# Running the last block's filter taps inside the last recurrence steps of a fused attention, GRU and convolution kernel

## The chip, the cores and the metric

The kernel runs on one core of one Trainium2 chip. The metric is the device time of one execution in microseconds; the time before is 1845.0 us, the median of three executions (1844.51 to 1854.32).

## What is computed

Four residual stages follow one another on an input `x` of shape (4, 512, 512) (batch, time, feature) with a conditioning vector of shape (4, 512). The first is an attention with 16 heads, the second a recurrence over the 512 time steps, the third and fourth depthwise causal convolutions whose four weights per feature are the conditioning vector's four rows:

```python
x = x + attention(x, cond)            # 16 heads, RMS norms, output projection
x = x + gru(cond, x)                  # 512 steps, one after the other
x = x + causal_conv(x, w=cond)        # 4 taps per feature
x = x + causal_conv(x, w=cond) + b    # 4 taps per feature, and a bias
```

The recurrence is sequential: a step needs the state of the step before. The two convolutions with their residuals are together one filter with seven taps per feature (k = 0 to 6), so output time t needs the sum of attention output and state at the times t-6 to t.

## The kernel before, in words

The time axis is cut into 16 blocks of 32 steps. One loop over the 512 steps (`for t in range(T)`) runs the recurrence, and beside it a list scheduler (`Queue`) writes the other work into the instruction streams in small pieces: the attention of later blocks, and the filter of the block before. The order in each engine's queue is the order in which the program emits instructions; nothing is moved afterwards. Each engine works its queue in that order.

**One recurrence step.** TensorE multiplies the state with the weights (L1250: 32 matmuls into X, 32 into Y). VectorE transposes X (L1264, tile TX) and adds (L1266, S). ScalarE takes the tanh (L1267, ZT), reseeds X for the next step (L1139) and forms D (L1270). VectorE transposes Y (L1276) and scans (L1277), ScalarE takes the second tanh (L1278), and VectorE's scans write the new state, A (L1287) in half and HS (L1288) in full precision. `prep` then makes the operands of the next step: BX on VectorE (L1149) and ScalarE (L1151), BY on GpSimd (L1150) and ScalarE (L1152), HH on GpSimd (L1154). Last, GpSimd adds the new state to the attention output X1 and writes column 6 + t % 32 of a history buffer `x2b` (L1292). `x2b` has 38 columns per row: six from the block before, and 32 of the block.

**The filter of a block** (`conv_tasks`). Task C1 has stages that `q_.head` emits at the start of a step, right behind `prep` and L1292 of the step before and in front of the step's own work on VectorE, ScalarE and GpSimd. `f1` (L1175) starts the sum in a tile `x4` with tap 0 and the bias: four ScalarE instructions, one for each group j of 128 features, which read columns 0 to 31 of `x2b`. Tap k then adds columns k to k+31, either on VectorE with one instruction for each group (`tap`, L1183), or on GpSimd with two (`tap_p`, L1190 and L1191). Tap k so reads column 31 + k last, which is the state of step 25 + k of the block. Task TX transposes the result on TensorE (L310, tile px), copies it on ScalarE to a tile `ob` (L1209) and sends it out with one DMA of 256 KB on SyncE's queue (L1210). `ob` is allocated with the tag of `x4`, and that tag has one buffer. The counter `cv` (one) lets C1 of a block start only when TX of the block before has been emitted.

For blocks 0 to 14 the filter is spread over the steps of the next block, all its taps on GpSimd (24 pairs). For block 15 there is no next block: its C1 is made behind the loop and flushed, with three groups' taps on VectorE (18 instructions) and one group's on GpSimd (6 pairs).

**The scheduler's limits.** A stage is emitted in a step if its planned cost fits into what is left of the engine's budget in that step (`DVE_B, ACT_B, POOL_B = 1130, 1900, 3300`), or if the whole budget of that engine is left. Tasks are looked at in the order of their priority: TX of block 14 comes ahead of C1 of block 15. A task's next stage comes at the earliest one step later.

Of the kernel before, what the change touches and what calls it, by code (L numbers as in the profile page):

```python
# [15 lines left out]
B, T, D, H = 4, 512, 512, 16  # L16
P = 128
NB = T // 32
# [12 lines left out]
PR = dict(LX=(86, 0), XH=(-226, 0), Q=(-27, 0), R=(-389, 0), ON=(-294, 0),  # L31
          TO=(-110, 0), WO=(-65, 0), GI=(-82, 0), C1=(130, 0),
          TX=(130, 0), LK=(159, 1.1), S=(4, 4.8), TP=(52, 4.7), AV=(115, 2.6))
# [138 lines left out]
def body(ctx, tc, x, cond, W_emb, b_emb, g_norm, W_qkv, g_q, g_k, W_out, W_ih, W_hh, b_ih, b_hh, L3_b, out):  # L172
# [13 lines left out]
    def pm(name):  # L186
        return pb.tile([P, 512], F32, name=name, tag="m", bufs=2)
# [128 lines left out]
    def lt(name, shape, dt=F32, bufs=1, tag=None):  # L316
        return lat.tile(shape, dt, name=name, tag=tag or name, bufs=bufs)
# [11 lines left out]
    q_ = Queue(dict(m=2, s=3, O=1, P=4, PT=4, xb=3, xhl=1, QS=3, q=1, o=1, gi=1, x1=3, L=3))  # L329
# [788 lines left out]
    f = lambda a: a.rearrange("p a k -> p (a k)")  # L1118
# [22 lines left out]
    def seedY(t):  # L1141
        nc.scalar.activation(Y, G[(t // 4) % 2][:, t % 4, 2, :], AF.Copy)
# [24 lines left out]
    def conv_tasks(i):  # L1167
        s = {}
        a = x2b[i % 2]

        def f1(jp):
            if jp == 0:
                s["x4"] = lt("x4", [P, D])
            for j in (2 * jp, 2 * jp + 1):
                nc.scalar.activation(s["x4"][:, 128 * j:128 * j + 128].rearrange("p (b t) -> p b t", b=4), a[:, 4 * j:4 * j + 4, 0:32],  # L1175
                                     AF.Identity, scale=VC[:, j, 0:1], bias=l3T[:, j:j + 1])

        def tap(k, jp, js=None):
            def g():
                x4 = s["x4"].rearrange("p (a t) -> p a t", t=32)  # L1180
                for j in js or (2 * jp, 2 * jp + 1):
                    J = slice(4 * j, 4 * j + 4)
                    nc.vector.scalar_tensor_tensor(x4[:, J, :], a[:, J, k:k + 32], VC[:, j, k:k + 1], x4[:, J, :], ALU.mult, ALU.add)  # L1183
            return g

        def tap_p(k, j):
            def g():
                tm = lt("tm", [P, 4, 32], bufs=2)
                o = s["x4"].rearrange("p (a t) -> p a t", t=32)[:, 4 * j:4 * j + 4, :]
                nc.gpsimd.tensor_scalar(tm, a[:, 4 * j:4 * j + 4, k:k + 32], VC[:, j, k:k + 1], 1.0, ALU.mult, ALU.mult)  # L1190
                nc.gpsimd.tensor_tensor(o, tm, o, ALU.add)  # L1191
            return g

        C1 = Task(f"C1{i}", prio=100 * i + PR["C1"][0],
                  stages=[[("ACT", 700, lambda jp=jp: f1(jp))] for jp in range(2)] + ([
                      [("Pool", 900, tap_p(k, j))] for k in range(1, 7) for j in range(4)] if i < NB - 1 else [
                      [("Pool", 900, tap_p(k, 3)), ("DVE", 526, tap(k, 0)), ("DVE", 300, tap(k, 1, (2,)))] for k in range(1, 7)]),
                  acq=["cv"], rel=["x1"])

        def toc(j):  # L1200
            def f():
                if j == 0:
                    s["px4"] = pm("px4")
                transpose4(s["px4"], s["x4"], (j,))
            return f

        def tos():
            ob = lt("ob", [P, D], tag="x4")
            nc.scalar.activation(ob, s["px4"], AF.Copy)  # L1209
            nc.sync.dma_start(out[:, 32 * i:32 * i + 32, :], ob)  # L1210

        TX = Task(f"TX{i}", prio=100 * i + PR["TX"][0], deps=[C1], acq=["m"], chunks=[(150, toc(j)) for j in range(4)], stages=[[("ACT", 480, tos)]], rel=["m", "cv"])
        return [C1, TX]

    q_.free["cv"] = 1
    CT = {}
# [6 lines left out]
    with tc.manual_schedule(engines={ENG.PE, ENG.DVE, ENG.Activation, ENG.Pool, ENG.SP}):  # L1223
        seed_first(0, 0)
        Bx, By, HH = prep(A, HS, 0)
        due = None
        for t in range(T):
            i = t // 32
            zt, d0 = ZT[t % 2], D0[t % 2]
            if t % 32 == 0:  # L1230
                if i == 0:
                    taps_()
                else:
                    q_.flush(CT.get(i - 2, []))
                    CT[i - 1] = conv_tasks(i - 1)
                    q_.add(CT[i - 1])
            if t % 4 == 0 and t + 4 < T:
                due = t // 4 + 1
            if due and due % 8 == 0 and (t % 4 == GI_T or all(u.done is not None and u.done <= q_.step for u in need[due // 8])):
                q_.flush(need[due // 8])  # L1240
                load_g(due)
                due = None
            elif due and due % 8:
                load_g(due)
                due = None
            q_.head(dict(DVE=DVE_B, ACT=ACT_B, Pool=POOL_B))

            def mm(dst, lhs, M, W, k, cols):
                for qq in range(4):
                    nc.tensor.matmul(dst[32 * qq:32 * qq + M, :], lhs, W[:, k, cols].rearrange("p g (j q s) -> p q g j s", j=4, q=4)[:, qq], start=False, stop=True,  # L1250
                                     skip_group_check=True)

            for k in range(4):
                mm(X, A[:, 4 * k:4 * k + 4, 1], 4, Wlo, k, slice(0, 2))
            for k in range(4):
                mm(X, Bx[:, k].rearrange("p s b -> p (s b)"), 8, Whi, k, slice(0, 2))
            if t == 0:
                seed_first(0, 1)
            for k in range(4):
                mm(Y, By[:, k].rearrange("p b s -> p (b s)"), 16, Wlo, k, slice(2, 3))  # L1260
            for k in range(4):
                mm(Y, By[:, k].rearrange("p b s -> p (b s)"), 16, Whi, k, slice(2, 3))
            TX = wk.tile([P, 8, 32], F32, name="TX", tag="TX", bufs=1)
            nc.vector.transpose(TX.rearrange("p a r -> p (a r)"), X)  # L1264
            S = wk.tile([P, 64], F32, name="S", tag="S", bufs=1)[:, 0:32]
            nc.vector.tensor_tensor(S.rearrange("p (a b) -> p a b", a=8), TX[:, :, 0:4], TX[:, :, 4:8], ALU.add)  # L1266
            nc.scalar.activation(zt[:, :, :, 2], S.rearrange("p (g a) -> p g a", g=2), AF.Tanh, scale=0.5 * IWS)  # L1267
            if 1 < t + 1 < T:
                seedX(t + 1)
            nc.scalar.activation(d0[:, :, 1], zt[:, 1, :, 2], AF.Copy, scale=-0.5, bias=0.5)  # L1270
            D1 = wk.tile([P, 16, 2], F32, name="D1", tag="D1")
            An = wk.tile([P, 16, 2], F16, name="A", tag="A")
            HSn = wk.tile([P, 16, 2], F32, name="HS", tag="HS")

            TY = wk.tile([P, 2, 4, 4, 4], F32, name="TY", tag="TY", bufs=2)
            nc.vector.transpose(TY.rearrange("p h j b k -> p j h (b k)"), Y.rearrange("p (j h r) -> p j h r", j=4, h=2))  # L1276
            nc.vector.tensor_tensor_scan(f(NN), f(zt[:, 0]), TY[:, 0].rearrange("p j b k -> p (j b k)"), 0.0, ALU.mult, ALU.add)  # L1277
            nc.scalar.activation(D1[:, :, 0], NN[:, :, 3], AF.Tanh, scale=0.5 * IWS)  # L1278
            nc.vector.scalar_tensor_tensor(D1[:, :, 1], zt[:, 1, :, 2], 1.0, HH, ALU.add, ALU.mult)
            if 1 < t + 1 < T:  # L1280
                seedY(t + 1)
            if t == 0:
                seed_first(1, 0)
                seed_first(1, 1)
            q_.pe(SLOT0 if t < NS0 else PE_SLOT, INS0 if t < NS1 else PE_INS, (PART, 1e9))
            keep_warm(-(-(WARM - q_.cols) // 384), pm("warm")[:, 0:384] if q_.free["m"] else None)
            nc.vector.tensor_tensor_scan(f(An), f(d0), f(D1), 0.0, ALU.mult, ALU.add)  # L1287
            nc.vector.tensor_tensor_scan(f(HSn), f(d0), f(D1), 0.0, ALU.mult, ALU.add)  # L1288
            A, HS = An, HSn
            if t + 1 < T:  # L1290
                Bx, By, HH = prep(A, HS, t + 1)
            nc.gpsimd.tensor_tensor(x2b[i % 2][:, :, 6 + t % 32], X1[i].rearrange("p (a t) -> p a t", t=32)[:, :, t % 32], HS[:, :, 1], ALU.add)  # L1292
            if t % 32 == 31 and i + 1 < NB:
                nc.gpsimd.tensor_scalar(x2b[(i + 1) % 2][:, :, 0:6], x2b[i % 2][:, :, 32:38], 1.0, 1.0, ALU.mult, ALU.mult)
            q_.step += 1
        ct = conv_tasks(NB - 1)
        q_.add(ct)
        q_.flush(ct)


_INS = ["x", "cond_2048", "L0_cond_W_emb", "L0_cond_b_emb", "L0_cond_g_norm", "L0_cond_W_qkv", "L0_cond_g_q",
# [20 lines left out]
```

## Time and profile before

| what | value |
|---|---|
| median of three executions | 1845.0 us |
| the profiled execution: its own time | 1849.01 us |
| its span in the trace | 1846.9 us |
| TensorE busy (matmul) | 1575.0 us, 85% |
| VectorE busy | 1237.8 us, 67% |
| ScalarE busy | 1200.5 us, 65% |
| GpSimd busy | 767.5 us, 42% |
| mean granted TensorE clock | 0.989 |
| last recurrence step: first matmul | 1828.41 us |
| its new state HS written | 1831.45 us |
| last VectorE tap ended | 1838.75 us |
| DMA of the last output block issued | 1840.15 us |

Busy time is counted for each engine by itself, and the engines run at the same time; a share of 85% does not say that this engine sets the end. Here the loop over the steps is a chain that goes through all engines, so the table's lower half matters more for this change: it shows the end of the program, where nothing but the last block's filter and its output is left. The times of the steps are counted from the span's start. In this profile step 506 (`t = T - 6`) has its first matmul at 1813.54 us, and the steps 507 to 511 at 1816.51, 1819.51, 1822.48, 1825.44 and 1828.41 us.

### The profile page before, as it was taken

The numbers are of one execution on the slowest core, as the hardware profiler recorded it, in microseconds if no ns is written. First come the engines' busy times: TensorE is split into PE (matmuls) and PEld (weight loads), VectorE is DVE, ScalarE is ACT, GpSimd is POOL, SyncE is SP. The second block draws the span as 40 slices with busy tenths as digits, with TensorE's granted clock in tenths as the row PEclk, the third lists the DMA queues.
The fourth block names the chain that finished last, engine by engine and source line by source line (L and its number), as shares of the span: only waits on it lengthen the run. The fifth ranks groups of instructions, "written<-read, shape, count | busy, mean of one in ns | idle before, by whom it ended". The sixth has DMA issues, their size and how long they took to land.

```text
span 1846.9 us, 116397 instructions
## 1 busy us (share of the span) xinstructions
PE 1575.0 (85%) x49019; PEld 1159.2 (63%) x49019; DVE 1237.8 (67%) x4774; ACT 1200.5 (65%) x4701; POOL 767.5 (42%) x2850
## 2 busy tenths in 40 slices
PE   4889988899998989898989999898989898987554
PEld 2444566666766767676666667676766676765442
DVE  4785467576767676777677676766666777665555
ACT  4664466767676767677776767676767677755543
POOL 1255023252535444443535353545444453434343
PEclk9989999999999999999999999999999999999998
DMA  5662011101010101010100111010101000011000
GB/s 175 224 209 116 21 54 28 41 17 34 17 35 19 35 27 44 18 30 25 28 24 24 29 46 30 19 35 17 36 13 35 17 25 25 18 28 29 18 12 16
DMA packets 68937, 78.26 MB, mean 42 GB/s; under 512 B 6560, under 2 KB 54720, under 8 KB 67776
## 3 DMA queue, kind: packets, MB, share of 16 engines
q1 hardware_dynamic: 68416, 70.82, 12.6%
q8 instruction: 387, 6.34, 1.5%
q14 instruction: 134, 1.10, 0.2%
HBM read 44.58 MB, written 26.21 MB: 38 GB/s over the span
## 4 chain that ended last, share of the span: by engine, by line
PE 43%; DVE 21%; ACT 19%; issue 7%; DMA 4%; POOL 4%; SPq 1%; ACTq 0%; DVEq 0%; POOLq 0%
PE X L1250 23%; DVE TX L1264 7%; ACT X L1139 6%; PE ps L457 5%; DVE A L1287 4%; PE Y L1250 4%; ACT D L1278 4%; DVE S L1266 3%; PE ptp L310 2%; PE pgi L590 2%; ACT PX L473 2%; ACT D L1270 2%; PE pkv L949 2%; PE po L501 1%; ACT ZT L1267 1%
## 5 line engine op out<-in xcount | busy, mean ns | idle before, releaser
L1150 POOL TENSOR_TENSOR BY<-HS,A 128x32 f16<-128x32 f32 x512 | 127.2, 248 | 854.7 <-DVE HS L1288 799.6
L1250 PE MATMUL X<-Wlo,A 128*4 128x256 f16 x8192 | 312.6, 272 | 158.7 <-DVE A L1287 150.1
L1267 ACT ACTIVATE ZT<-S 128x32 f32<-128x32 f32 x512 | 133.3, 260 | 425.6 <-DVE S L1266 425.0
L1264 DVE STREAM_TRANSPOSE TX<-X 128x256 f32<-128x256 f32 x512 | 230.4, 450 | 257.0 <-PE X L1250 256.8
L1250 PEld LDWEIGHTS <-A 128*4 128x4 f16 x8192 | 151.9, 83 | 263.9 <-DVE A L1287 221.5
L1250 PE MATMUL X<-Whi,BX 128*8 128x256 f16 x8192 | 314.9, 273 | 0.9 <-issue 0.8
L1250 PEld LDWEIGHTS <-BY 128*16 128x16 f16 x16384 | 276.2, 90 | 35.4 <-issue 13.3
L1250 PE MATMUL Y<-Wlo,BY 128*16 128x128 f16 x8192 | 208.9, 219 | 11.6 <-POOL BY L1150 7.2
L1250 PE MATMUL Y<-Whi,BY 128*16 128x128 f16 x8192 | 209.9, 219 | 2.8 <-issue 2.4
L1250 PEld LDWEIGHTS <-BX 128*8 128x8 f16 x8192 | 180.8, 86 | 49.7 <-ACT BY L1152 3.9
L1139 ACT ACTIVATE X<-G 128x256 f32<-128x256 f32 x510 | 201.7, 396 | 5.3 <-DMA G<-GD 4.4
L473 ACT ACTIVATE PX<-ps,nb,rqs 128x512 f32<-128x512 f32 x256 | 195.4, 764 | 9.4 <-DVE nb L465 7.0
L1287 DVE TENSOR_TENSOR_SCAN A<-D,D 128x32 f16<-128x32 f32 x512 | 115.6, 226 | 122.9 <-ACT D L1278 121.9
L464 DVE TENSOR_REDUCE mx<-ps 128x1 f32<-128x512 f32 x256 | 174.6, 684 | 22.1 <-PE ps L457 22.0
L1277 DVE TENSOR_TENSOR_SCAN N<-ZT,TY 128x64 f32<-128x64 f32 x512 | 150.0, 293 | 58.7 <-ACT ZT L1267 7.8
L1191 POOL TENSOR_TENSOR x<-tm,x 128x128 f32<-128x128 f32 x366 | 166.6, 455 | 31.0 <-POOL tm L1190 0.6
L1276 DVE STREAM_TRANSPOSE TY<-Y 128x128 f32<-128x128 f32 x512 | 158.5, 310 | 17.5 <-PE Y L1250 7.7
L310 PE MATMUL ptp<-ident,PX 128*128 128x128 f32 x1024 | 165.2, 281 | 1.4 <-ACT PX L473 0.6
L501 PEld LDWEIGHTS po<-V,PT 128*32 128x32 f32 x8192 | 107.6, 111 | 77.9 <-issue 70.0
L501 PE MATMUL po<-V,PT 128*32 128x32 f32 x8192 | 147.9, 199 | 5.7 <-issue 4.9
L493 ACT ACTIVATE PT<-ptp 128x512 f32<-128x512 f32 x248 | 143.7, 582 | 11.0 <-PE ptp L310 10.9
L1151 ACT ACTIVATE BX<-A 128x16 f16<-128x16 f16 x512 | 110.8, 216 | 61.0 <-DVE A L1287 1.5
(268 smaller groups left out, 3074.5 us busy)
## 6 DMA issues: line engine op xcount, KB each, us to landing
GD<-gs SPq DMA_DIRECT2D x45, 256.0 KB
G<-GD SPq DMA_DIRECT2D x512, 16.0 KB
G<-GD SPq DMA_DIRECT2D x512, 8.0 KB
xp<-in_x_dram SPq DMA_DIRECT2D x16, 256.0 KB
xb<-in_x_dram SPq DMA_DIRECT2D x16, 256.0 KB
xhl<-XD SPq DMA_DIRECT2D x32, 128.0 KB
out_dram<-ob SPq DMA_DIRECT2D x16, 256.0 KB
wst<-in_L_cond_W_qkv_dram SPq DMA_DIRECT2D x6, 512.0 KB
```

The costliest lines, as they stand in the source:

```text
L310: nc.tensor.transpose(dst[:, 128 * j:128 * j + 128], src[:, 128 * j:128 * j + 128], ident)
L464: nc.vector.tensor_reduce(s["mx"][:, h:h + 1], s[("s", j, q)], AX.X, ALU.max)
L473: nc.scalar.activation(pe_, s[("s", j, q)], AF.Exp, bias=s["nb"][:, h:h + 1], scale=s["rqs"][:, h:h + 1], accum_out=s["ls"][:, h:h + 1])
L501: nc.tensor.matmul(s["po"][32 * b:32 * b + 32, 32 * h:32 * h + 32], s["PT"][h][:, kt, 32 * b:32 * b + 32], V[:, 4 * b + kt, 32 * h:32 * h ...
L1139: nc.scalar.activation(X.rearrange("p (g c) -> p g c", g=2), G[(t // 4) % 2][:, t % 4, 0:2, :], AF.Copy)
L1191: nc.gpsimd.tensor_tensor(o, tm, o, ALU.add)
L1250: nc.tensor.matmul(dst[32 * qq:32 * qq + M, :], lhs, W[:, k, cols].rearrange("p g (j q s) -> p q g j s", j=4, q=4)[:, qq], start=False, st ...
L1264: nc.vector.transpose(TX.rearrange("p a r -> p (a r)"), X)
L1267: nc.scalar.activation(zt[:, :, :, 2], S.rearrange("p (g a) -> p g a", g=2), AF.Tanh, scale=0.5 * IWS)
L1276: nc.vector.transpose(TY.rearrange("p h j b k -> p j h (b k)"), Y.rearrange("p (j h r) -> p j h r", j=4, h=2))
L1277: nc.vector.tensor_tensor_scan(f(NN), f(zt[:, 0]), TY[:, 0].rearrange("p j b k -> p (j b k)"), 0.0, ALU.mult, ALU.add)
L1287: nc.vector.tensor_tensor_scan(f(An), f(d0), f(D1), 0.0, ALU.mult, ALU.add)
```

## The change

Only block 15's filter is changed. Its C1 is put into the scheduler at step 506 (26 of the block) in place of behind the loop. There `f1` becomes one stage of four instructions. One stage follows for each of the taps 1 to 5: groups 0 and 1 on VectorE, groups 2 and 3 on GpSimd. Tap 6 has groups 0, 1 and 2 on VectorE and group 3 on GpSimd. With one stage for each step, `f1` comes at the head of step 506, taps 1 to 5 at the heads of steps 507 to 511, and tap 6 is flushed behind the loop.

```diff
-        C1 = Task(f"C1{i}", prio=100 * i + PR["C1"][0],
-                  stages=[[("ACT", 700, lambda jp=jp: f1(jp))] for jp in range(2)] + ([
-                      [("Pool", 900, tap_p(k, j))] for k in range(1, 7) for j in range(4)] if i < NB - 1 else [
-                      [("Pool", 900, tap_p(k, 3)), ("DVE", 526, tap(k, 0)), ("DVE", 300, tap(k, 1, (2,)))] for k in range(1, 7)]),
-                  acq=["cv"], rel=["x1"])
+        if i < NB - 1:
+            st = [[("ACT", 700, lambda jp=jp: f1(jp))] for jp in range(2)] + [[("Pool", 900, tap_p(k, j))] for k in range(1, 7) for j in range(4)]
+        else:
+
+            st = [[("ACT", 1400, lambda: (f1(0), f1(1)))]] + [
+                [("DVE", 526, tap(k, 0)), ("Pool", 900, tap_p(k, 2)), ("Pool", 900, tap_p(k, 3))] for k in range(1, 6)] + [
+                [("DVE", 526, tap(6, 0)), ("DVE", 300, tap(6, 1, (2,))), ("Pool", 900, tap_p(6, 3))]]
+        C1 = Task(f"C1{i}", prio=100 * i + PR["C1"][0], stages=st, acq=["cv"], rel=["x1"])
...
+            if t == T - 6:
+                CT[NB - 1] = conv_tasks(NB - 1)
+                q_.add(CT[NB - 1])
             q_.head(dict(DVE=DVE_B, ACT=ACT_B, Pool=POOL_B))
...
-        ct = conv_tasks(NB - 1)
-        q_.add(ct)
-        q_.flush(ct)
+        q_.flush(CT[NB - 1])
```

## The prediction

> **What bounds the kernel now.** I read the chain of waits first. Up to the last step it is the recurrence, about 2.97 us a step and through every engine; behind it the chain, asked for the last 22 us, is the filter of the last block on VectorE, then its output (columns: start us, length us, what):
>
> ```profile
> 1828.41 1.07 PE X L1250 x32
> ...
> 1831.52 4.11 DVE x L1183 x11
> 1835.63 0.41 issue
> 1836.04 1.06 DVE x L1183 x3
> 1837.10 0.24 issue
> 1837.34 0.90 DVE x L1183 x2
> 1838.23 0.14 issue
> 1838.37 1.14 PE px L310 x4
> 1839.53 0.60 ACT ob L1209
> ```
>
> So 7.23 us of taps (18 on VectorE, 1831.52 to 1838.75) stand bare at the end. That bounds the gain: it can't be more than 0.4% of the time. A difference of 0.5% (9.2 us) is about what a measurement of this kernel can tell from no change.
>
> Next the timeline, at single records of the taps (start us, length us):
>
> ```profile
> 1837.34 0.62 DVE L1183 SCALAR_TENSOR_TENSOR x<-x2b,VC,x 128x128 f32<-128x128 f32 x1
> 1838.41 0.34 DVE L1183 SCALAR_TENSOR_TENSOR x<-x2b,VC,x 128x128 f32<-128x128 f32 x1
> ```
>
> The first ran beside a GpSimd add (L1191), the second with GpSimd idle. Beside GpSimd's multiply a tap takes 0.45 us. Alone, taps follow one another in 0.27 us; beside GpSimd's pairs (0.925 us each) two fit into a pair, 0.46 us each.
>
> **What the change removes.** Behind the loop only tap 6 is left. In the clock of the old trace: GpSimd's last column (L1292) is written at 1831.77. VectorE's three taps then start at about 1831.83, 2.20 and 2.66 (the first beside GpSimd's multiply, the second beside its add, the third mostly with GpSimd idle) and end at 1833.05; GpSimd's pair ends at about 1832.7. The old transposes ended 0.74 us behind the last tap (1838.75 to 1839.49), the new ones then end at 1833.79. The gain is 1839.49 - 1833.79 = **5.7 us**. Copy and output behind it are the same. The transposes in the middle of the loop, at full clock, took 0.67 us for four against 1.12 at the end, so if the clock is still up another 0.2 goes; I leave it out.
>
> **What it adds at step 506.** f1 goes to ScalarE's queue right behind block 14's copy to `ob` (planned 480 + 1400 of 1900, so it fits), and in front of the step's tanh. f1 writes `x4`, which lives in the one buffer that `ob` has. It must wait until block 14's output DMA has read `ob`. Before, f1 came 16.6 us after that DMA's issue (1814.37 to 1830.98), and nothing waited. The timeline shows copy and tanh; the DMA view, asked from the issue at 1814.37 for 12 us (slices of 0.3 us), shows the transfer:
>
> ```profile
> 1813.76 0.58 ACT L1209 ACTIVATE ob<-px 128x512 f32<-128x512 f32 x1
> 1815.35 0.26 ACT L1267 ACTIVATE ZT<-S 128x32 f32<-128x32 f32 x1 [1.01 <-DVE S L1266]
> ```
> ```profile
> DMA  0000271301212222210000002000000000000001
> ```
>
> Packets move until slice 18, 5.6 us after the issue. The same transfer at the very end is waited for, so its completion is seen. This line is from the waits of SyncE's queue (us, times, longest):
>
> ```profile
> SPq L1315 <- DMA out_dram<-ob: 5.2, 1, 5.2
> ```
>
> Issued at 1840.15 and 0.55 long, plus 5.2: completion 5.75 us after issue. So f1 can start at 1814.37 + 5.75 = 1820.12. Four instructions at a pitch of 0.385 (1830.98, 1831.37, 1831.75, 1832.13 in the old tail) hold ScalarE until 1821.7, where the tanh stood ready for 1815.35. Everything else of the step hangs on that tanh: **+6.35 us**. Bounds: without any wait f1 would start when column 31 is there (1814.37) and end at 1815.95, +0.6; with the slowest of the 16 output transfers in this trace, whose stretch has packets until 8.3 us after issue (other loads among them), +9.0. I take 5.75, since both transfers with nothing beside them (blocks 14 and 15) end in the same slice.
>
> The Trainium skill, page "DMA: Bandwidth & Descriptors", section "Anatomy of one DMA — SWDGE (gpsimd) path", gives a transfer as about 2 us fixed plus bytes over 436 GB/s, for GpSimd's queue. By that 256 KB would take 2.6 us, step 506 would lose 3.2, and the sum would come to +1.3 us. The trace has the duration for SyncE's queue, so 5.75 is used.
>
> **What it adds at steps 507 to 511.** Two taps each go to VectorE's queue between BX (L1149) and the transpose of X. Step 508 in the old trace:
>
> ```profile
> 1819.51 0.61 PE L1250 MATMUL X<-Wlo,A 128*4 128x256 f16 x16 [1.24 <-DVE A L1287]
> 1819.60 0.17 DVE L1149 TENSOR_TENSOR BX<-HS,A 128x16 f16<-128x16 f32 x1
> 1820.12 0.24 POOL L1292 TENSOR_TENSOR x2b<-x,HS 128x16 f32<-128x16 f32 x1
> 1820.61 0.45 DVE L1264 STREAM_TRANSPOSE TX<-X 128x256 f32<-128x256 f32 x1 [0.83 <-PE X L1250]
> ```
>
> The 0.83 us of idle VectorE looks like room for two taps. But the tap reads the column that L1292 writes, and that ends at 0.85 us into the step, 0.25 ahead of the transpose. A tap added here waits on GpSimd, and behind it in VectorE's queue stands the transpose, which the whole step waits for. First tap at about 0.93 (0.45 long, beside GpSimd's multiply), second at 1.30 (0.62, beside the add), transpose at about 1.86 in place of 1.10: **+0.76 us a step**. Bounds: nothing, if they were done in the idle time; +1.0, if both take 0.62 and none of it overlaps. I take 0.76, from the tail's own records of the same mix.
>
> GpSimd's two pairs run from 0.87 to 2.72 us into the step; its next work (BY) starts 3.2 us into it (1822.71 against 1819.51). It fits, with half a microsecond to spare that a longer step widens. SyncE's queue gets nothing; f1's wait does not hold it up, for block 14's DMA is ahead of it.
>
> Step 507 is another case. TensorE last worked at 1815.31 (its filler matmul) and would idle until 1816.51 + 6.35: 7.5 us. An idle of 3.04 us earlier in this trace shows what follows; the timeline there, and two pieces of the chain, one behind that idle and one of a usual step:
>
> ```profile
> 235.42 1.02 PE L1250 MATMUL X<-Wlo,A 128*4 128x256 f16 x16 [3.04 <-DVE A L1287]
> ```
> ```profile
> 235.42 1.88 PE X L1250 x32
> ...
> 1795.70 1.07 PE X L1250 x32
> ```
>
> The granted clock was 0.50 there until about 238.7, and the product took 1.88 in place of 1.07. So step 507 loses 0.81, and the taps (until 1.85) are hidden behind the longer product: +0.81 in place of 0.76. Were step 508 slow as well, it would cost 0.05 more.
>
> The Trainium skill, "TensorE: Matmul & The Clock Gate", section "HAM oscillation", says that idle gaps over about 3.4 us lower the clock; here 3.04 us was enough. By the rule the final transposes (idle some 2.2 us) would run at full clock, 0.2 us off the sum; the old tail, where the clock fell 2.5 us into the idle time, leaves it open.
>
> **Sum.** -5.7 + 6.35 + 0.81 + 4 x 0.76 (3.04) = **+4.5 us**. Against the profiled execution that is 1849.0 to 1853.5; that execution lay 4.0 us above the median of the three, so against the median: **1849.5 us**, slower by 0.24%, less than a measurement can tell.
>
> **Rivals.**
>
> - The transfer is no wait (f1 gets another buffer after all, or its data are long read). Then +0.6 at step 506, no low clock, 5 x 0.76: 0.6 + 3.8 - 5.7 = -1.3, **1843.7 us**. For it: the planner counts f1 as fitting. Against it: one tag, one buffer, and an output transfer issued in the same step. This is the faster side; if the taps hid too it would be 1840.
> - The taps are hidden (they start sooner, or VectorE runs them at the pitch of 0.27). Hidden wholly in steps 508 to 511: 6.35 + 0.81 - 5.7 = +1.5, **1846.5 us**. Against it: L1292's end at 0.85.
> - The transfer lands late, at ScalarE's cost: with 8.3 us after issue, +2.6 more, **1852.1 us**. For it: transfers with loads of G beside them show packets for 7 us and more. Against it: the last load of G was issued at 1808. This mechanism makes the change slower by over 0.5% only if the landing takes over 10.4 us, 4.7 more than measured.
> - The change does not do what it says: if f1 missed ScalarE's budget at 506, all stages come one step later and two taps are left at the end. Then the tanh of step 507 (1818.32) would wait until 1821.7, 3.4 in place of 6.35; one slowed step less (-0.76), one more tap at the end (+1.3, two pairs of GpSimd bare): **1847.1 us**.
>
> **How the numbers follow.** Forecast 0.62, no wait 0.10, hidden taps 0.10, late landing 0.13, a step later 0.05. The likeliest one's own range is 1847.5 to 1851.5. The range over the cases reaches from 1843.5 (no wait) to 1853.5 (late landing, and 1 us for the executions' spread). All cases lie within 0.5%: same 0.93. Faster by that much is above what the tail holds: 0.02. Slower: late landing beyond 10.4 us, or a median disturbed as one of the three was (1854.32): 0.05.
>
> **What will show it.** The profile after should have, near 1815, an idle ScalarE of some 5 us in front of L1175 whose releaser is the DMA of `ob`; a TensorE idle of about 7.5 us and a clock of 0.50 behind it; in steps 508 to 511 a length near 3.7 us with the transpose of X right behind two taps; three taps behind the last step, and the span's end about 10 us after their start. I am wrong if L1175 follows L1209 at once, or if these steps keep their 2.97 us.

## The result, and the profile after

The changed kernel takes 1853.19 us (median of 20 executions) against 1848.14 us of the kernel before (20 executions, in the same sessions): a ratio of 1.0025, 95% interval 1.0015 to 1.0034, so slower by 4.6 us (2.8 to 6.3); the medians themselves lie 5.05 us apart. The forecast was +4.5 us, 0.24%, and had called that less than a measurement can tell; with 20 executions of each it could be told.

Single executions of one kernel spread over more than 10 us, because what lies ahead of step 505 varies: its first matmul was at 1810.57 us in the profile of before, at 1809.16, 1810.87 and 1808.94 in three profiles of the changed kernel, and anywhere from 1805.54 to 1816.74 over the twelve profiles of this document. So I compare **the closing stretch**, from the first matmul of step 505 to the end of the span. It comes out alike in the three profiles of the changed kernel (42.54, 42.53 and 42.36 us); before was profiled once. The change does nothing ahead of it:

| closing stretch, us | before | after | difference | forecast |
|---|---|---|---|---|
| step 506 | 2.97 | 9.51 | +6.54 | +6.35 |
| step 507 | 3.00 | 4.14 | +1.14 | +0.81 |
| steps 508, 509, 510 | 2.97, 2.96, 2.97 | 4.14, 4.49, 4.14 | +3.87 | +2.28 |
| step 511, to its scan A | 2.70 | 3.34 | +0.64 | +0.76 |
| scan A to the last copy to ob | 8.42 | 2.50 | -5.92 | -5.70 |
| whole (36.33 and 42.54) | | | +6.2 | +4.5 |

(The copy to ob begins 7.37 and 7.31 us before the end, and step 505 is 2.97 us long in both.)

The chain of waits of the changed kernel, over this stretch (start us, length us, what):

```profile
1812.95 5.89 DMA out_dram<-ob
...
1818.95 1.65 ACT x L1175 x4
1820.60 0.15 ACT ZT L1273
...
1821.64 1.88 PE X L1256 x32
1823.52 0.88 PE Y L1256 x32
...
1824.50 0.33 DVE TY L1282
...
1825.78 1.88 PE X L1256 x32
1827.66 0.89 PE Y L1256 x32
...
1842.58 0.35 DVE x L1183
...
1843.31 0.56 DVE x L1183
...
1843.91 0.45 PE px L310 x2
1844.39 0.60 ACT ob L1212
```

The seven microseconds of taps at the end have shrunk to 1.3. In their place stand the output DMA of block 14, which was not on the old chain, and steps in which TensorE's product is 2.76 us long (X, then Y), where X alone with 1.07 us carried the old chain. The timeline names the two idle times:

```profile
1818.95 1.65 ACT L1175 ACTIVATE x<-x2b,VT,VC 128x128 f32<-128x128 f32 x4 [6.02 <-DMA out_dram<-ob]
1821.64 1.02 PE L1256 MATMUL X<-Wlo,A 128*4 128x256 f16 x16 [7.75 <-DVE A L1293]
```

ScalarE stood for 6.02 us in front of f1, and TensorE idled for 7.75 us. The clock is read from stretches of 3.41 us, laid so that the granted clock changes at their ends (columns: length, TensorE busy and its instructions, granted clock, DMA share, GB/s):

```profile
1816.94:1820.36 3.42, 0.00 (x0) 0.50 0.10 40
1820.36:1823.77 3.41, 2.13 (x52) 0.50 0.00 0
...
1830.60:1834.01 3.41, 2.48 (x57) 0.50 0.01 2
1834.01:1837.42 3.41, 3.01 (x65) 0.50 0.02 5
1837.42:1840.84 3.42, 1.91 (x66) 1.00 0.00 0
```

Half clock from 1816.94 to 1837.42: not for step 507 alone, but into step 510. That is the main difference to the forecast.

### The profile page after: what moved, and what is told of

The parts are those of the page before. It is cut to its first block, busy times and chain, and to the rows that moved or that the text cites. A ratio compares the mean times of both kernels' runs of the same rounds, so it can differ in the third digit from the quotient of the medians.

```text
span 1851.7 us, 116400 instructions
## 1 busy us (share of the span) xinstructions
PE 1580.7 (85%) x49019; PEld 1162.8 (63%) x49019; DVE 1236.0 (67%) x4769; ACT 1201.3 (65%) x4701; POOL 774.1 (42%) x2860
## 4 chain that ended last, share of the span: by engine, by line
PE 46%; DVE 21%; ACT 19%; issue 6%; POOL 4%; DMA 3%; SPq 1%; DVEq 0%; ACTq 0%; POOLq 0%
PE X L1256 24%; DVE TX L1270 7%; ACT X L1139 6%; PE ps L457 5%; DVE A L1293 4%; PE Y L1256 4%; ACT D L1284 4%; DVE S L1272 3%; PE pgi L590 2%; PE pkv L949 2%; PE ptp L310 2%; ACT PX L473 2%; ACT D L1276 2%; PE po L501 2%; ACT ZT L1273 1%
```

## The experiments

The theory: what is lost comes from f1's wait for the output transfer (one buffer for `x4` and `ob`), from the half clock that the wait leaves behind, and from taps that wait for the history column. The rivals: the taps by themselves make the steps long; or GpSimd beside VectorE does.

### Giving ob a buffer of its own

```diff
-            ob = lt("ob", [P, D], tag="x4")
+            ob = lt("ob", [P, D])
```

> The changed kernel, with a buffer of its own for ob, so that x4 of the last block need not wait for the output transfer of the block before. Measure: the closing stretch, from the first matmul of step 505 to the end of the span, 36.3 us before and 42.5 us after. Theory (the wait for the transfer, and the low clock behind it, are the loss): no idle ScalarE in front of f1, clock 1.00 throughout, step 506 longer by 0.6, steps 507 to 511 longer by 0.64 to 0.76 each, stretch 34.2 to 34.8, so 1.5 to 2 us faster than before. Rival (the taps between the steps are the loss, the transfer is not): steps 507 to 510 stay at 4.1 to 4.5 us and the stretch is 36.5 or more.

Measured: 1844.79 us against 1848.45, ratio 0.9985 (0.9968 to 1.0002), which by itself does not tell it from no change. The closing stretch is 34.27 us, 2.1 less than before and 8.3 less than in the changed kernel. Step 506 takes 3.56, steps 507 to 510 take 3.60 or 3.61, step 511 takes 3.33 to its scan A; no clock below 1.00 in these steps, no wait of ScalarE. In the closing stretch one tag turns a loss of 6.2 us into a gain of 2.1. A step at full clock, VectorE and then GpSimd:

```profile
1821.82 0.73 DVE L1183 SCALAR_TENSOR_TENSOR x<-x2b,VC,x 128x128 f32<-128x128 f32 x2 [0.59 <-POOL x2b L1298]
1822.47 0.43 DVE L1270 STREAM_TRANSPOSE TX<-X 128x256 f32<-128x256 f32 x1
...
1823.47 0.51 DVE L1283 TENSOR_TENSOR_SCAN N<-ZT,TY 128x64 f32<-128x64 f32 x1
```
```profile
1823.38 0.45 POOL L1191 TENSOR_TENSOR x<-tm,x 128x128 f32<-128x128 f32 x1
```

VectorE does wait 0.59 us for GpSimd's column, and the transpose comes 1.52 us into the step in place of 1.10: +0.42. The other 0.22 of the step is the scan of N, 0.51 us in place of 0.29, and GpSimd's second add runs beside it.

### Filling the wait with matmuls

```diff
             keep_warm(-(-(WARM - q_.cols) // 384), pm("warm")[:, 0:384] if q_.free["m"] else None)
+            if t == T - 6:
+                keep_warm(36, pm("warm")[:, 0:384])
```

> The changed kernel, with 36 filler matmuls of 384 columns more on TensorE in step 506, some 5.8 us that lie in the time in which the step waits for the transfer. Theory (steps 507 to 510 are long because the clock fell in the idle time): clock 1.00 throughout, these steps 3.6 to 3.7 us in place of 4.1 to 4.5, ScalarE's wait of 6 us unchanged, closing stretch 40.1 us against 42.5. Rival (they are long because of the taps): 4.1 us and more each, 42.5.

Measured in one execution: ScalarE's wait is still 6.03 us and step 506 9.52, but TensorE idles for only 1.91 us, the clock stays at 1.00, and steps 507 to 510 take 3.60, 3.61, 3.71 and 3.60. Closing stretch 40.25, 2.3 less than the changed kernel, as the theory had it. Of the 8.3 us between the changed kernel and the one with the buffer, the low clock is 2.3 and the wait 6.0.

### Moving only f1

```diff
-            st = [[("ACT", 1400, lambda: (f1(0), f1(1)))]] + [
-                [("DVE", 526, tap(k, 0)), ("Pool", 900, tap_p(k, 2)), ("Pool", 900, tap_p(k, 3))] for k in range(1, 6)] + [
-                [("DVE", 526, tap(6, 0)), ("DVE", 300, tap(6, 1, (2,))), ("Pool", 900, tap_p(6, 3))]]
+            st = [[("ACT", 1400, lambda: (f1(0), f1(1)))]] + [[]] * 5 + [
+                [("Pool", 900, tap_p(k, 3)), ("DVE", 526, tap(k, 0)), ("DVE", 300, tap(k, 1, (2,)))] for k in range(1, 7)]
```

> The changed kernel with only f1 moved forward to step 506; taps 1 to 6 come behind the loop as they did before, three groups on VectorE and one on GpSimd. Theory (at half clock the taps of steps 507 to 510 are hidden behind the longer products, and clock and wait cost all of it): the 6 us wait stays, the clock is 0.50, the steps behind it are as long as in the changed kernel, 4.1 us, without any tap, and the closing stretch is 36.3 + 6.5 + 5 x 1.15 = 48.6. Rival (the taps make these steps long): 3.8 us each for the longer product of X alone, 46.8 in all.

Measured in one execution: closing stretch 44.06, which neither had forecast. Step 507 is 4.14 us long without any tap, exactly as with them, and its transpose of X comes at 1.93 us in both: at half clock the taps cost nothing. But the steps behind it are back at 2.97, since the clock returned after one step:

```profile
1814.52:1817.94 3.42, 0.00 (x0) 0.50 0.02 7
1817.94:1821.35 3.41, 3.16 (x65) 0.50 0.00 0
1821.35:1824.76 3.41, 1.76 (x65) 1.00 0.02 5
```

So the theory lacked a rule for when the clock returns. The times from fall to return were 20.48 us (changed kernel), 6.83 (here), and 3.41 at 235 us in the profile of before: six, two and one times 3.41. That gave the next two experiments.

### More filler behind the wait

```diff
+            if T - 6 < t < T - 1:
+                keep_warm(4, pm("warm")[:, 0:384])
```

> The changed kernel with four filler matmuls more on TensorE in each of the steps 507 to 510, behind the wait, so that TensorE has hardly a gap between the steps while the clock is low. The looks so far have the clock change only at times that lie whole multiples of 3.41 us apart (fall to return: 20.5, 6.8 and 3.4 us). Theory (the clock is decided at the end of each stretch of 3.41 us by how busy TensorE was in it; 72% was too little and 89% enough): the clock returns one or two such stretches after step 507 begins, two steps at the most are long (about 4.4 with the fillers), closing stretch 40.4 to 41.8. Rival (the clock comes back a fixed time after the work, or needs full-rate steps): low for four steps again, 42.5 to 43.5.

Measured in one execution: 10.24 us from fall to return, three times 3.41; the stretch whose end brought the clock back had TensorE busy for all of its 3.41 us. Step 507 takes 4.37, step 508 3.36, the closing stretch is 40.76. With more work on TensorE the end was 1.8 us shorter, as the theory had it. This is one execution, and the number of long steps also varies between executions of one kernel (below), so the fillers' own share in it is not shown.

### The clock in further executions

> The changed kernel once more, for a second look at the clock. Theory (stretches of 3.41 us that run freely, against steps of 4.14 us at half clock with a gap of about 1 us in each): the time from fall to return is again a multiple of 3.41 us, but not the same one of necessity; one to five steps are long, closing stretch 39.9 to 43.7. Rival (the taps keep the clock down): 20.5 us and four long steps again, 42.5.

> The kernel with only f1 moved forward, once more. In its first look the clock fell and came back 6.83 us later, two stretches of 3.41 us, so that only step 507 was long (4.14 us) and the closing stretch was 44.1 us. Theory (the clock is decided at the ends of stretches that run freely through the whole execution, by how busy TensorE was in each; where they lie against the steps is chance): fall to return again a multiple of 3.41 us, one to five steps long, closing stretch 44.1 to 48.7. Rival (without taps the clock always returns after one step): 6.83 us and 44.1 again.

> The changed kernel, third look. Two looks had 20.48 us from fall to return and four long steps. Theory (chance of the stretches' place): a multiple of 3.41 us, one to five long steps, closing stretch 39.9 to 43.7; another number than six would show that four long steps are no property of the kernel. Rival (the taps keep the clock down for these four steps): 20.48 us and 42.5 again.

Measured: the changed kernel has again 20.48 us and four long steps (42.53) in one execution, and 17.07 us and three in another (4.15, 4.14, 4.49, then 3.62; 42.36). With f1 alone again 6.8 us and one long step (43.95). Every time is a multiple of 3.41 us, and the number differs between executions of one kernel, so the rival of a fixed four is out. That f1 alone needed just two stretches in both of its executions fits that rival as well as chance. The busy share of the stretch at whose end the clock returned was between 83% and 100% in the six executions in which the clock fell at step 506. No stretch of 74% or less brought it back in these six:

```profile
1826.21:1829.63 3.42, 2.54 (x57) 0.50 0.02 5
1829.63:1833.04 3.41, 3.16 (x65) 0.50 0.00 0
1833.04:1836.45 3.41, 1.76 (x65) 1.00 0.03 7
```

(the execution with three long steps). A step of 4.14 us at half clock has a gap of about 1.0 us at its end. A stretch that takes in one whole gap reaches some 72%, one that lies between two gaps 93%.

The busy share does not decide it everywhere. In the attention early in the program, the second profile with f1 alone has three stretches in a row with TensorE busy 3.21, 3.42 and 3.29 us (179.65 to 189.89 us) that left the clock at 0.50, and a fourth of 3.41 us that brought it back. In the profile with more filler behind the wait the clock fell at 185.66 us after a stretch with 2.30 us of work. What else counts there stays open; the theory is shown for the last steps only.

### Leaving out GpSimd's taps

The kernel with the buffer, without taps 1 to 5 of groups 2 and 3, so with part of the filter missing:

```diff
-                [("DVE", 526, tap(k, 0)), ("Pool", 900, tap_p(k, 2)), ("Pool", 900, tap_p(k, 3))] for k in range(1, 6)] + [
+                [("DVE", 526, tap(k, 0))] for k in range(1, 6)] + [
```

> As the kernel with a buffer of its own for ob, but taps 1 to 5 of groups 2 and 3 on GpSimd are left out (work is missing, the output is not the reference's), so that VectorE's taps run with GpSimd idle. Theory (VectorE's taps and its scan of N are slowed by GpSimd's taps beside them): two taps in 0.54 us, the scan at 0.29 in every step, steps 507 to 511 about 3.35 us, closing stretch 33.0. Rival (only the wait for the history column costs): steps as long as with GpSimd's taps, 3.6 to 3.7, stretch 34.5.

Measured in one execution: closing stretch 32.55, steps 507 to 510 3.27 to 3.28.

```profile
1826.23 0.61 DVE L1183 SCALAR_TENSOR_TENSOR x<-x2b,VC,x 128x128 f32<-128x128 f32 x2 [0.61 <-POOL x2b L1298]
1826.77 0.44 DVE L1270 STREAM_TRANSPOSE TX<-X 128x256 f32<-128x256 f32 x1
...
1827.76 0.29 DVE L1283 TENSOR_TENSOR_SCAN N<-ZT,TY 128x64 f32<-128x64 f32 x1
```

The wait for the column and the taps behind it cost a step 0.31 us, GpSimd's work beside them another 0.32 (0.10 in the taps, 0.22 in the scan).

### VectorE's taps one step later

On top of the buffer: f1 for groups 2 and 3 in step 506 and for 0 and 1 in step 507, VectorE's tap k in step 507 + k, GpSimd's as before.

```diff
-            if jp == 0:
+            if "x4" not in s:
...
+            V2 = lambda k: [("DVE", 526, tap(k, 0))]
+            P2 = lambda k: [("Pool", 900, tap_p(k, 2)), ("Pool", 900, tap_p(k, 3))]
+            st = [[("ACT", 700, lambda: f1(1))], [("ACT", 700, lambda: f1(0))] + P2(1)] + [
+                V2(k - 1) + P2(k) for k in range(2, 6)] + [
+                V2(5) + [("DVE", 526, tap(6, 0)), ("DVE", 300, tap(6, 1, (2,))), ("Pool", 900, tap_p(6, 3))]]
```

> A buffer of its own for ob; VectorE's taps 1 to 5 come one step later than GpSimd's, so that the column they read last was written a step before; f1 in two halves, groups 2 and 3 in step 506 and groups 0 and 1 in step 507. Behind the loop VectorE has five taps (k = 5 for two groups, k = 6 for three). Theory (a tap on VectorE costs a step nothing once it need not wait for GpSimd's column, and f1 costs nothing in halves): X's transpose at 1.1 us into the steps 507 to 511 in place of 1.5, steps 2.97 to 3.2 (what is over is the scan of N beside GpSimd's second pair), closing stretch 31.3 to 31.9 us (before 36.3, with only the buffer 34.3). Rival (the two taps cost the step their own length wherever they stand, since GpSimd's BY, HH and column now run beside them and slow or delay them): steps stay near 3.5, stretch 33.5 or more.

Measured: 1844.75 us against 1850.77, ratio 0.9965 (0.9953 to 0.9977); closing stretch 32.45, 3.9 less than before. f1 in halves costs nothing (step 506: 2.97), and the transpose of X stands at 1.09 or 1.10 us in steps 507, 508, 509 and 511 (1.35 in step 510). But the steps are 3.0 to 3.6 long, not 2.97 to 3.2, and the closing stretch lies between what theory and rival had: GpSimd's adds now meet other instructions of the step.

```profile
1818.17 0.45 POOL L1191 TENSOR_TENSOR x<-tm,x 128x128 f32<-128x128 f32 x1
1818.24 0.43 DVE L1274 TENSOR_TENSOR S<-TX 128x32 f32<-128x32 f32 x1
...
1819.06 0.48 POOL L1191 TENSOR_TENSOR x<-tm,x 128x128 f32<-128x128 f32 x1
1819.21 0.36 DVE L1287 SCALAR_TENSOR_TENSOR D<-ZT,HH 128x16 f32<-128x16 f32 x1
```

S takes 0.43 in place of 0.19, and D 0.36 in place of 0.15.

### Three groups on VectorE, one on GpSimd, one step later

As the last, with `tap(k, 1, (2,))` beside `tap(k, 0)` on VectorE and `tap_p(k, 3)` alone on GpSimd in each stage.

> As the kernel with VectorE's taps one step later, but three groups on VectorE and one on GpSimd, so that GpSimd has one pair a step and is done before the scan of N. Behind the loop VectorE has six taps. Theory (GpSimd's second pair costs 0.2 us a step by the scan of N): N at 0.29 us in every step, X's transpose at 1.1 to 1.3, steps 2.97 to 3.15, the end up to 0.5 longer for the sixth tap, closing stretch 30.6 to 31.8. Rival (three taps don't fit into 0.83 us): X's transpose at 1.4 or later, steps 3.3, stretch 32.5.

Measured: 1844.31 us against 1850.77, ratio 0.9965 (0.9952 to 0.9978); closing stretch 31.77, 4.6 less than before, the shortest. Three taps (0.93 to 0.94 us) fit, with the transpose at 1.10; N stays at 0.29. Steps 508 to 510 are still 3.2 long, a little over the forecast of 3.15, as S takes 0.43 beside the one add that is left. The two last kernels are faster than before, by 0.35% each, and their closing stretch is 10 to 11 us shorter than that of the changed kernel; between each other their times don't differ.

## Why the prediction was right, point by point

- **The tail** (-5.7): right, -5.92. Three taps behind the last step, timed from the taps' own records and from the old end. The 0.2 more is of the size that the prediction had set aside for final transposes at full clock; here two of the four ended before the clock fell.
- **f1 waits for the output transfer** (+6.35): right, +6.54. The transfer was issued at 1812.95 and ScalarE went on at 1818.95, 6.0 us where 5.75 was read from the waits at the old end. The buffer of its own is the proof: step 506 went from 9.51 to 3.56. The formula of the Trainium skill ("DMA: Bandwidth & Descriptors", "Anatomy of one DMA — SWDGE (gpsimd) path"), which is for GpSimd's queue, gives 2.6 us, an estimate that would have missed more than half of it.
- **The clock falls in the idle time** (+0.81 at step 507): the mechanism was right, but two sizes were off. I read only the product of X (1.88 against 1.07) from the old record at 235 us. Y is slowed as well, 0.88 us behind X, so VectorE's transpose TY waits for it: +1.14. And the step "Were step 508 slow as well, it would cost 0.05 more" failed twice over: a step at half clock costs 1.14 to 1.53 in place of 0.76, and there were four of them, or three. The longest, step 509, holds 0.35 us that are not TensorE's: there the trace has TY wait 0.60 us, ended by ScalarE's reseed of X, where in the steps beside it it waits 0.25 us for TensorE; why only there is open. I had taken the return after 3.4 us from a place with attention matmuls between the products; in the last steps there are none.
- **The clock's rule.** The Trainium skill, "TensorE: Matmul & The Clock Gate", Part 1, describes a window of 4096 cycles, 3413 ns, that runs freely. The runs agree: the times from fall to return are 1, 2, 3, 5 and 6 times 3.41 us, and two of the falls in the profile of before, at 235.21 and 1832.65 us, lie 1597.44 us apart, 468 times 3.4133. I had cited the page for idle gaps and not for this.
- **Taps between the steps** (+0.76): nearly right in size at full clock, 0.63 to 0.64, and wrong in its parts. In the changed kernel itself only step 511 ran at full clock and shows it; in the steps before, the long product hid the taps. The wait for GpSimd's column is there (0.59 to 0.60 us in each step), but the transpose moves by 0.42 only. The rest is a cost that I had not listed: GpSimd's add beside the scan of N.
- **The sum** (+4.5): the whole-kernel ratio has it at +4.6, 2.8 to 6.3. The closing stretch, with less noise, has +6.0 to +6.2. Against the first profile's +6.2 the forecast was short by 1.7 us; the long steps' part of the miss is 1.9 (0.33 at step 507, 1.59 behind it), and the other terms give a little back. That 4.5 and 4.6 agree so closely is therefore in part luck: the path was right, and the clock's term was too small.

What stays open: in which share of executions three, four or another number of steps are long. Three profiles have four, four and three.

## What to carry to other kernels

Work that is moved earlier also moves towards the last use of its buffer: look at who held that buffer last, and how long its transfer takes to complete, before counting idle time as free. A stall in a loop of alternating engines costs more than its length when TensorE's clock falls in it, so price it by full steps at half clock. Where a tap must wait for another engine's late write, one step of delay hides the wait, though the tap's neighbours on the other engine may then run beside other instructions and slow those.

## What the runs showed of the hardware

- TensorE's clock was low for whole multiples of 3.41 us each time it returned. In the last steps and behind them it fell after stretches of that length in which TensorE was busy for 1.29 us or less (38%, f1 alone at 1831.59 us), and stayed up with 1.57 us (46%, steps with ob's own buffer) or 1.76 us (52%, usual steps). There it returned after 83% or more, and did not return after 74%. A loop whose steps have a gap of 1 us in 4.1 stayed at half clock for 20 us. In the attention early in the program, with other matmuls, these shares do not hold: 94% to 100% left the clock low, and 67% (2.30 us) did not keep it up.
- GpSimd's two-input add slows VectorE's instructions with two inputs from SBUF beside it: N 0.29 to 0.51 us, S 0.19 to 0.43, D 0.15 to 0.36, a tap 0.34 to 0.62. The transpose of X, whose input is in PSUM, took 0.43 to 0.45 with an add beside it and without. The Trainium skill, "GPSIMD Engine Reference", section "Key points", names this contention for instructions with two SBUF inputs; the rows agree and give its size.
